# Cross-attention over 1024 context rows: the values' projection applied after the probabilities instead of before

## The chip, the cores and the metric

The kernel runs on one core of a Trainium2 chip. The time is device microseconds of one execution. Before the change the median of three runs is 3087.88 us (3087.36 to 3091.29). A core has five engines with instruction queues of their own: PE (matrix products; its loads of stationary operands are listed as PEld), DVE (vector), ACT (scalar functions), POOL (general) and SP (here it issues transfers). Work from one engine to another is ordered by semaphores. PE writes into PSUM (eight banks of 128 partitions by 512 float32 numbers); DVE and ACT take the results out.

## The reference, cut to what matters

A network of twelve blocks on x (16 batches of 64 tokens by 256). The tenth, the one changed, lets the 64 latents of a batch attend to 1024 context rows of 192 numbers and to the 64 latents themselves, in 4 heads of 64:

```python
def _L3_xattn_ref(x, latents, mask, ln_x_g, ln_x_b, ln_l_g, ln_l_b, qn_g, kn_g, Wq, Wkv, Wlkv, Wo, bo):
    ...
    xn = layernorm(x, ln_x_g, ln_x_b)          # x: the context, 16 x 1024 x 192
    ln = layernorm(latents, ln_l_g, ln_l_b)    # 16 x 64 x 256
    q = ln @ Wq.T
    kv = jnp.concatenate([xn @ Wkv.T, ln @ Wlkv.T], axis=1)
    k, v = (kv[..., :INNER], kv[..., INNER:])  # INNER = 256
    q, k, v = (split_heads(q), split_heads(k), split_heads(v))
    qn = rmsnorm(q, qn_g) * SCALE
    kn = rmsnorm(k, kn_g)
    attn = jnp.einsum('bhid,bhjd->bhij', qn, kn)
    ...                                        # masked context keys are left out
    attn = jax.nn.softmax(attn, axis=-1)
    out = jnp.einsum('bhij,bhjd->bhid', attn, v)
    out = out.transpose(0, 2, 1, 3).reshape(b, m, INNER)
    ...                                        # times Wo, plus bo; added to the stream
```

## The kernel before, in words

All numbers are float32. Blocks follow one another; `ffn2` (from line 2711) stands ahead of the changed block `xattn3` (from line 1689), `attn3` behind it. `context_weights` (line 1659) is called at the start of `ffn2`: it fetches the 192 x 512 weight wx of keys and values, forms bx (the layernorm's shift times the weight, one row repeated on all partitions), scales the weight by the layernorm's gain and takes its mean over rows away, so that a context row times wx, times the row's inverse deviation, plus bx is the projection of the normalised row. The inverse deviations of all context rows, `rctx`, were left by an earlier block.

`xattn3` loops over the 16 batches. One pass handles the softmax and values of batch b and prepares the keys and values of batch b+1:
- `scores` multiplies the 64 queries of each head with transposed keys `kT`, in three pieces (512 keys, then the 128 latents' places, then the other 512). `least` (DVE) adds the mask and finds the minimum; ACT takes the exponential with its sum and then multiplies by the reciprocal sum (`pr`, 128 x 1152 for each of two pairs of heads c).
- `project(b, j)`, four groups j a batch, makes keys and values of 2 x 128 context rows: two products with 128 stationary rows and two with 64 (the other context columns; the two halves of the array side by side), each 512 wide: 256 for keys, 256 for values. DVE (scalar_tensor_tensor) takes each half out into `kk` and `vv`, times rctx plus bx.
- `square` (ACT), `roots` (a sum on DVE, then two instructions on POOL, lines 1761 and 1762) and `scale` (DVE) normalise each group of keys; p0, p1, p2 and late are the states of groups 0 to 3.
- `keys_T` transposes a group on PE (tile `ptk`) and ACT copies it to kT; group 3 of batch b+1 is transposed only after the first scores of the next pass. `latents` (product `pkl` once per two batches, copies on POOL, line 1787) and `latents_T` do the same for the latents' own keys and values.
- `probs_T` transposes the probabilities on PE (`ptp`, two banks for each c) and ACT copies them to `pT`; `last_T` (`pto`) does so for the latents' places. `values` multiplies `vv` with `pT`: 9 key tiles x 4 heads, products 64 wide. ACT copies the result `po` to `oT`, and `output` multiplies with Wo for two batches at once, in passes of even b from 2 on, and after the loop.

The order of work on PE, DVE and ACT is the program's own: instructions recorded through `self.mm`, `self.tr`, `dve` and `act` carry an order dependency on the one before them on that engine (`in_order`, line 189). POOL's and SP's orders, and DVE instructions of the next block, are placed by the scheduler of the framework. Helpers record all of them, so the profile shows line 205 for products, 208 for transposes and 72 for DVE and ACT. Passes 1 to 3 also make the queries of later batches. `mid` holds 7 PSUM banks in rotation, `ps_o` one.

## Time and profile before

| | |
|---|---|
| median of the runs | 3087.88 us |
| profiled execution | 3099.52 us, span 3097.5 us, mean clock of PE 0.963 |
| PE, DVE, ACT, POOL busy, share of the span | 94%, 63%, 43%, 24% |
| changed block | from 2433.3 us (first pkv) to 2825.0 us (last sum into X) |
| its passes, from first scores to first scores | 29.5 us for b = 0; 24.1 to 24.7 for b = 1 to 3; 21.7 to 22.8 after |
| last pass, from first scores | 18.7 us |

A row of the order of time or of the chain of waits gives start, length, engine, line, operation, output <- inputs, partitions x elements and how many instructions are merged. Idle time before an instruction and what ended it stand in brackets. In a row of groups the last columns are total busy time, mean duration in ns, and idle time before with its releaser. In a row of windows come the length, then for PE, PEld, DVE, ACT and POOL the busy time with the number of instructions, then PE's granted clock, the share of the transfer engines and GB/s. Instructions of DVE and ACT overlap a little: one of 0.68 us lets the next start after some 0.6.

### The profile page before, as it was taken

The numbers are of one execution on the slowest core, as the hardware profiler recorded it, in microseconds if no ns is written. First come the engines' busy times: TensorE is split into PE (matmuls) and PEld (weight loads), VectorE is DVE, ScalarE is ACT, GpSimd is POOL, SyncE is SP. The second block draws the span as 40 slices with busy tenths as digits, with TensorE's granted clock in tenths as the row PEclk, the third lists the DMA queues.
The fourth block names the chain that finished last, engine by engine and source line by source line (L and its number), as shares of the span: only waits on it lengthen the run. The fifth ranks groups of instructions, "written<-read, shape, count | busy, mean of one in ns | idle before, by whom it ended". The sixth has DMA issues, their size and how long they took to land.

```text
span 3097.5 us, 66367 instructions
## 1 busy us (share of the span) xinstructions
PE 2901.7 (94%) x27980; PEld 1819.7 (59%) x27980; DVE 1952.1 (63%) x4054; ACT 1329.3 (43%) x3041; POOL 731.1 (24%) x817
## 2 busy tenths in 40 slices
PE   8999999899999999977988999998989899998888
PEld 4666666666455554456874555546976455455677
DVE  6888886523766664972127877767884677775521
ACT  3555554511554451002324444438851255554322
POOL 1000002400110001014430100024871355552132
PEclk9999999999999999988999999998998999999889
DMA  2100000013223323026762222101111111110143
GB/s 77 32 32 31 24 22 19 17 32 101 64 73 101 99 60 83 1 69 242 295 235 69 73 71 76 60 22 40 49 58 31 64 58 65 62 55 15 61 145 125
DMA packets 75824, 225.28 MB, mean 73 GB/s; under 512 B 17415, under 2 KB 30586, under 8 KB 68616
## 3 DMA queue, kind: packets, MB, share of 16 engines
q1 hardware_dynamic: 47536, 115.57, 12.0%
q0 software_dynamic: 21744, 99.34, 9.4%
q10 hardware_dynamic: 6248, 6.14, 0.7%
q8 instruction: 221, 3.62, 0.5%
q14 instruction: 75, 0.61, 0.1%
HBM read 210.09 MB, written 14.49 MB: 73 GB/s over the span
## 4 chain that ended last, share of the span: by engine, by line
PE 80%; DVE 10%; ACT 4%; DMA 2%; issue 2%; POOL 2%; SPq 0%; DVEq 0%; POOLq 0%; ACTq 0%
PE pss L205 15%; PE o L205 13%; PE pu L205 8%; PE pd L205 7%; PE psp L205 6%; PE pkv L205 5%; PE pst L208 4%; PE psc L205 3%; PE po L205 2%; DVE h L72 2%; PE psq L205 2%; PE psy L205 1%; PE pg L205 1%; PE ptp L208 1%; DVE nm L72 1%
## 5 line engine op out<-in xcount | busy, mean ns | idle before, releaser
L205 PE MATMUL pss<-cT,qw 128*32 128x256 f32 x8192 | 367.7, 385 | 18.7 <-ACT pr L72 18.6
L72 DVE TENSOR_REDUCE nm<-pss 128x2 f32<-128x512 f32 (+1 forms) x384 | 309.3, 861 | 82.7 <-PE pss L205 82.7
L205 PE MATMUL o<-pT,cx 128*64 128x512 f32 (+3 forms) x1088 | 351.7, 576 | 0.0
L72 ACT ACTIVATE pr<-pss,nmm 128x256 f32<-128x256 f32 x512 | 234.8, 485 | 161.5 <-DVE nmm L72 161.5
L205 PEld LDWEIGHTS pss<-cT,qw 128*32 128x32 f32 x8192 | 203.5, 109 | 148.4 <-ACT pr L72 26.1
L205 PEld LDWEIGHTS o<-pT,cx 128*64 128x64 f32 (+1 forms) x1088 | 134.3, 163 | 188.4 <-issue 161.8
L222 POOL TENSOR_SCALAR rs<-mv 128x8 f32<-128x8 f32 (+3 forms) x50 | 9.7, 194 | 974.7 <-DVE mv L238 511.7
L72 ACT ACTIVATE pr<-pr,sm 128x256 f32<-128x256 f32 x256 | 109.1, 497 | 203.9 <-DVE sm L72 203.9
L205 PE MATMUL pkv<-wx,cT 128*128 128x512 f32 (+1 forms) x512 | 193.1, 630 | 0.6 <-issue 0.6
L72 DVE TENSOR_SCALAR pr<-pr,sm 128x256 f32<-128x256 f32 (+1 forms) x384 | 170.1, 485 | 6.6
L1555 POOL TENSOR_TENSOR h<-h,cb 128x1024 f32<-128x1024 f32 x64 | 149.5, 2376 | 38.2 <-DVE h L72 37.2
L205 PE MATMUL pd<-wd,hT 128*128 128x256 f32 x656 | 151.5, 382 | 2.6 <-DVE hT L2754 1.4
L72 DVE TENSOR_TENSOR_SCAN h<-dA,pb 128x512 f32<-128x512 f32 x128 | 146.5, 1202 | 10.8 <-PE pb L205 7.4
L72 DVE STREAM_TRANSPOSE pT<-pr 128x1024 f32<-128x1024 f32 x128 | 151.8, 1224 | 2.2
L2531 DVE TENSOR_SCALAR y<-pd,row 128x256 f32<-128x256 f32 x39 | 18.8, 483 | 207.5 <-PE pd L205 161.8
L72 ACT ACTIVATE pr<-pss,nm 128x1024 f32<-128x1024 f32 x128 | 142.7, 1115 | 11.4 <-DVE nm L72 8.7
L208 PE MATMUL pst<-ident,pr 128*128 128x128 f32 x1024 | 140.6, 280 | 5.8 <-DVE sm L72 1.9
L208 PEld LDWEIGHTS pst<-ident,pr 128*128 128x128 f32 x1024 | 109.8, 141 | 61.5 <-ACT pT L72 26.5
L72 ACT COPY pT<-pst 128x512 f32<-128x512 f32 x128 | 75.0, 586 | 163.2 <-PE pst L208 163.2
L205 PEld LDWEIGHTS pd<-wd,hT 128*128 128x128 f32 x656 | 122.0, 190 | 30.3 <-DVE hT L2754 6.2
L205 PEld LDWEIGHTS pkv<-wx,cT 128*128 128x128 f32 (+1 forms) x512 | 64.4, 188 | 118.5 <-issue 92.6
L1762 POOL TENSOR_TENSOR rnk<-rnk,mhalf 128x8 f32<-128x8 f32 (+1 forms) x84 | 130.0, 1548 | 7.0
(570 smaller groups left out, 5803.3 us busy)
## 6 DMA issues: line engine op xcount, KB each, us to landing
cT<-in_ctxT SPq DMA_DIRECT2D x32, 768.0 KB, 4.9
cx<-in_ctxP SPq DMA_DIRECT2D x32, 768.0 KB, 4.4
cT<-in_ctxT SPq DMA_DIRECT2D x32, 512.0 KB, 4.1
cT<-in_ctxT SPq DMA_DIRECT2D x64, 256.0 KB, 5.1
offb<-d_off SPq DMA_DIRECT2D x16, 576.0 KB, 3.7
cb<-d_C SPq DMA_DIRECT2D x16, 512.0 KB, 3.9
wu<-in_L_ffn_w POOLq DMA_DIRECT2D x8, 1024.0 KB
wd<-in_L_ffn_w POOLq DMA_DIRECT2D x8, 1024.0 KB
```

The source lines that it names most:

```text
L72: ins = getattr(self.engine, op)(*args, **kwargs)
L205: self.in_order(self.nc.tensor.matmul(out, lhsT=lhsT, rhs=rhs, start=start, stop=stop))
L208: self.in_order(self.nc.tensor.transpose(out, in_, self.ident))
L222: nc.gpsimd.tensor_scalar(t[:p, :n], in_, scale, eps, ALU.mult, ALU.add)
L1555: nc.gpsimd.tensor_tensor(hs[i], hs[i], cbs[hf, g], ALU.mult)
L1762: nc.gpsimd.tensor_tensor(r, r, self.mhalf[:, : n * H], ALU.pow)
L2531: nc.vector.tensor_scalar(y[:, i, :], po[:, i * D : (i + 1) * D], weight[:, g + i : g + i + 1], None, ALU.mult)
```

## The change

Keys are projected as before, 256 wide. Values of the context are not projected. Since the softmax sum of (rctx times row times weight plus shift) is (sum of probability times rctx times row) times weight plus shift, the transposed probabilities are multiplied by rctx when they are taken out of PSUM (`probs_T`, now on DVE), and multiply the raw context rows, loaded once more in row order (`cx`, `load_cx`), in `values` (128 of the 192 columns) and `others` (64 columns, the key tiles alternating between two halves of the array). This happens one pass later, for batch b-1: `values` ahead of the second projection group, `others` after the last one. ACT copies the result of all heads to `oc`, and `heads` applies each head's 192 x 64 weights for two batches at once, adds the latents' own values (whose shift was taken away in `latents`, a subtraction on POOL) times their probabilities (`pls`), and ACT adds the shift `vb` while copying to `oT`. `vb` is made in `context_weights` by four products one column wide.

```diff
         bx = own.tile([P, 512], F32, name="bx")
-        self.wx, self.bx = wx, bx
+        vb = own.tile([P, 2], F32, name="vb")
+        self.wx, self.bx, self.vb = wx, bx, vb
         mean = own.tile([P, P], F32, name="mean")
...
             nc.scalar.copy(bx, pb)
+            pv = pool.tile([P, 512], F32, tag="m", name="pvb")
+            for c in range(2):
+                for k, n in enumerate((P, C1)):
+                    ch = slice(D + c * P, D + (c + 1) * P)
+                    self.mm(pv[:, c : c + 1], wx[:n, k, ch], self.col(f"{L}_ln_x_b", k, p=n), k == 0, k == 1)
+            nc.scalar.copy(vb, pv[:, :2])
             for k in range(2):
...
             ps_o = es.enter_context(tc.tile_pool(name=f"{L}ps_o", bufs=1, space=PSUM))
-            wx, bx = self.wx, self.bx
+            wx, bx, vb = self.wx, self.bx, self.vb
...
             qb = one.tile([P, 2, B, TQ], F32, name="qb")
-            oT = one.tile([P, 2, N], F32, name="oT")
-            kks, vvs = [], []
+            kks = []
             for i in range(2):
-                for lst, nm in ((kks, "kk"), (vvs, "vv")):
-                    x = one.tile([P, KT, H, 64], F32, name=f"{nm}{i}")
-                    nc.gpsimd.memset(x[64 - 64 * i : 128 - 64 * i, NKC], 0.0)
-                    lst.append(x)
-            ctxs, offs, kvl, st = {}, {}, {}, {}
+                x = one.tile([P, KT, H, 64], F32, name=f"kk{i}")
+                nc.gpsimd.memset(x[64 - 64 * i : 128 - 64 * i, NKC], 0.0)
+                kks.append(x)
+            ctxs, cxs, offs, kvl, vls, pTs, pls, ocs, oTs, st = ({} for _ in range(10))
...
             def square(x, n):
...
             def load(b):
...
                     ctxs[b] = self.load_ctxT(two, b)
+            def load_cx(b):
+                cxs[b] = two.tile([P, NKC, C], F32, tag="cx", name="cx")
+                nc.sync.dma_start(out=cxs[b], in_=a["ctxP"][b])
...
             def load_off(b):
...
                     act.copy(kvl[0], pl)
-                for i, dst in enumerate((kks[b % 2], vvs[b % 2])):
-                    nc.gpsimd.tensor_copy(
-                        dst[own, NKC].rearrange("p h d -> p (h d)"), kvl[0][own, i * D : (i + 1) * D]
-                    )
+                    vl = vls[b // 2] = two.tile([P, H, 64], F32, tag="vl", name="vl")
+                    nc.gpsimd.tensor_tensor(vl.rearrange("p h d -> p (h d)"), kvl[0][:, D:], bx[:, D:], ALU.subtract)
+                nc.gpsimd.tensor_copy(kks[b % 2][own, NKC].rearrange("p h d -> p (h d)"), kvl[0][own, :D])
                 return kks[b % 2][:, NKC : NKC + 1], 1
...
             def project(b, j):
...
                 c0, c1 = ctxs[b]
-                kk, vv = kks[b % 2], vvs[b % 2]
-                pp = [mid.tile([P, 512], F32, tag="m", name="pkv") for _ in range(2)]
+                kk = kks[b % 2]
+                pp = [mid.tile([P, 512], F32, tag="m", name="pk") for _ in range(2)]
                 for n in range(2):
                     jj = 4 * n + j
-                    self.mm(pp[n], c0[:, jj * P : (jj + 1) * P], wx[:, 0, :], True, False)
+                    self.mm(pp[n][:, :D], c0[:, jj * P : (jj + 1) * P], wx[:, 0, :D], True, False)
                 for n in range(2):
                     r = slice(n * 64, (n + 1) * 64)
-                    self.mm(pp[n], c1[r, j * P : (j + 1) * P], wx[r, 1, :], False, True)
+                    self.mm(pp[n][:, :D], c1[r, j * P : (j + 1) * P], wx[r, 1, :D], False, True)
                 for n in range(2):
-                    for i, dst in enumerate((kk, vv)):
-                        jj = 4 * n + j
-                        dve.scalar_tensor_tensor(
-                            dst[:, 2 * j + n].rearrange("p h d -> p (h d)"),
-                            pp[n][:, i * D : (i + 1) * D],
-                            self.rctx[:, b, jj : jj + 1],
-                            bx[:, i * D : (i + 1) * D],
-                            ALU.mult,
-                            ALU.add,
-                        )
+                    jj = 4 * n + j
+                    dve.scalar_tensor_tensor(
+                        kk[:, 2 * j + n].rearrange("p h d -> p (h d)"),
+                        pp[n][:, :D],
+                        self.rctx[:, b, jj : jj + 1],
+                        bx[:, :D],
+                        ALU.mult,
+                        ALU.add,
+                    )
                 return kk[:, 2 * j : 2 * j + 2], 2
...
             def turn(pt, at, x):
...
-            def last_T(prs):
+            def last_T(b, prs):
+                pls[b] = two.tile([P, 2, P], F32, tag="pl", name="pl", bufs=3)
                 pt = mid.tile([P, 512], F32, tag="m", name="pto")
...
                     turn(pt, c, prs[c][:, S:])
-                act.copy(st["pT"][:, :, NKC, :], pt[:, : 2 * P].rearrange("p (c q) -> p c q", c=2))
+                act.copy(pls[b], pt[:, : 2 * P].rearrange("p (c q) -> p c q", c=2))
...
             def scores(b, lo, hi):
...
-            def probs_T(c, pr):
+            def probs_T(b, c, pr):
+                if c == 0:
+                    pTs[b] = two.tile([P, NKC, 2, P], F32, tag="pT", name="pT")
+                r = self.rctx[:, b, :].rearrange("p (n j) -> p j n", n=2)
                 for jh in range(2):
...
                         turn(pt, j, pr[:, (4 * jh + j) * P : (4 * jh + j + 1) * P])
-                    act.copy(st["pT"][:, c, 4 * jh : 4 * jh + 4, :], pt.rearrange("p (j q) -> p j q", q=P))
-            def values(b, c):
-                for j in range(KT):
-                    for h in range(2):
-                        u = (h ^ c) * TQ
-                        self.mm(
-                            st["po"][h * 64 : (h + 1) * 64, c * TQ : (c + 1) * TQ],
-                            vvs[b % 2][:, j, 2 * c + h, :],
-                            st["pT"][:, c, j, u : u + TQ],
-                            j == 0,
-                            j == KT - 1,
-                        )
+                    dve.tensor_tensor(
+                        pTs[b][:, 4 * jh : 4 * jh + 4, c, :].rearrange("p (j n) q -> p j n q", n=2),
+                        pt.rearrange("p (j n q) -> p j n q", j=2, n=2),
+                        bc(r[:, 2 * jh : 2 * jh + 2], 3, P),
+                        ALU.mult,
+                    )
+            def tile_of(b, k):
+                return cxs[b][:, 4 * (k % 2) + k // 2], pTs[b][:, k].rearrange("p c q -> p (c q)")
+            def values(b):
+                st["o"] = ps_o.tile([P, 2, 2 * P], F32, tag="o", name="o")
+                for k in range(NKC):
+                    cx, pT = tile_of(b, k)
+                    self.mm(st["o"][:, 0, :], cx[:, :P], pT, k == 0, False)
+            def others(b):
+                for k in range(NKC):
+                    cx, pT = tile_of(b, k)
+                    self.mm(st["o"][k % 2 * 64 : k % 2 * 64 + 64, 1, :], cx[:, P:], pT, False, k >= NKC - 2)
+                if b % 2 == 0:
+                    ocs[0] = one.tile([P, 2, 2 * H // 2, 2, TQ], F32, tag="oc", name="oc")
+                act.copy(ocs[0][:, :, :, b % 2, :], st["o"].rearrange("p i (h q) -> p i h q", q=TQ))
+            def heads(m):
+                po = mid.tile([P, 512], F32, tag="m", name="poh")
+                po = po[:, : 2 * P].rearrange("p (c q) -> p c q", c=2)
+                for c in range(2):
+                    for i in range(2):
+                        for hh in range(2):
+                            h = 2 * c + hh
+                            self.mm(
+                                po[hh * 64 : hh * 64 + 64, c, :],
+                                wx[:, i, D + h * 64 : D + (h + 1) * 64],
+                                ocs[0][:, i, 2 * c + (hh ^ c)].rearrange("p b q -> p (b q)"),
+                                c == 0 and i == 0,
+                                False,
+                            )
+                for c in range(2):
+                    for bb in range(2):
+                        for hh in range(2):
+                            u = (hh ^ c) * TQ
+                            self.mm(
+                                po[hh * 64 : hh * 64 + 64, c, bb * TQ : (bb + 1) * TQ],
+                                vls[m][:, 2 * c + hh, :],
+                                pls[2 * m + bb][:, c, u : u + TQ],
+                                False,
+                                c == 1 and bb == 1,
+                            )
+                oT = oTs[m] = two.tile([P, 2, P], F32, tag="oT", name="oT")
+                for c in range(2):
+                    act.activation(oT[:, c], po[:, c], AF.Identity, bias=vb[:, c : c + 1])
...
             def output(t):
...
                 for c in range(2):
-                    self.mm(ps[:, :D], oT[:, c, t * P : (t + 1) * P], wo[:, c, :], c == 0, c == 1)
+                    self.mm(ps[:, :D], oTs[t][:, c, :], wo[:, c, :], c == 0, c == 1)
                 dve.tensor_tensor(self.X[:, t, :], self.X[:, t, :], ps[:, :D], ALU.add)
...
             for b in range(B):
...
                 load(b + 2)
+                load_cx(b)
                 load_off(b + 1)
...
                 sums = self.small.tile([P, 2], F32, tag="sums", name="sums")
-                st["po"] = ps_o.tile([P, 2 * TQ], F32, tag="o", name="po")
                 pss = scores(b, 0, 512)
...
                     p0, lat = roots(*p0), roots(*lat)
+                if b > 0:
+                    values(b - 1)
                 dve.reciprocal(sums[:, 0:1], sums[:, 0:1])
...
                     late = project(b + 1, 3)
-                st["pT"] = one.tile([P, 2, KT, P], F32, tag="pT", name="pT")
-                probs_T(0, prs[0])
+                if b > 0:
+                    others(b - 1)
+                probs_T(b, 0, prs[0])
                 if more:
                     keys_T(b + 1, 0, act.copy)
-                last_T(prs)
+                last_T(b, prs)
                 if more:
                     late = square(*late)
-                probs_T(1, prs[1])
+                probs_T(b, 1, prs[1])
                 if more:
...
                     keys_T(b + 1, 1, act.copy)
+                if b % 2 == 0 and b > 0:
+                    heads(b // 2 - 1)
                 if 1 <= b <= 3:
                     scale(*q)
-                values(b, 0)
-                values(b, 1)
                 if more:
...
                     scale(*late)
-                act.copy(oT[:, :, b * TQ : (b + 1) * TQ], st["po"].rearrange("p (c q) -> p c q", c=2))
                 if 1 <= b <= NT:
                     nc.gpsimd.tensor_tensor(self.X[:, b - 1, :], self.X[:, b - 1, :], row, ALU.add)
+            values(B - 1)
+            others(B - 1)
+            heads(NT - 1)
             output(NT - 1)
```

## The prediction

> **What bounds the kernel now.** I read the page first (PE busy 94%), then the busy time by windows over the changed block (2433 to 2825 us), then its chain of waits, then the order of time inside one batch. Two neighbouring batches by windows (length; then busy PE, PEld, DVE, ACT, POOL; clock), with batch 0:
>
> ```profile
> 2458.90:2488.40 29.50, 25.36 (x174) 12.93 (x173) 21.12 (x55) 13.71 (x24) 15.73 (x18) 0.87 0.14 48
> ...
> 2628.40:2651.20 22.80, 22.55 (x173) 11.34 (x172) 16.45 (x44) 12.24 (x21) 10.95 (x14) 1.00 0.18 61
> 2651.20:2672.90 21.70, 21.64 (x173) 11.21 (x172) 15.56 (x40) 13.16 (x24) 10.66 (x11) 1.00 0.18 66
> ```
>
> PE is full at full clock; the pair takes 44.5 us. The chain of waits from batch 4 on is nearly all PE:
>
> ```profile
> 2652.83 2.78 PE pkv L205 x8
> 2655.61 1.24 PE pss L205 x16
> 2656.85 8.92 PE pkv L205 x24
> 2665.77 1.02 PE ptp L208 x8
> ```
>
> So a projection group is 2.78 or 2.97 us of path. But behind the last of them PE meets DVE and POOL just in time (order of time; brackets are idle time and its releaser):
>
> ```profile
> 2646.94 0.68 DVE L72 TENSOR_TENSOR kk<-kk,rnk 128x512 f32<-128x512 f32 x1
> ...
> 2647.76 0.63 PE L208 MATMUL ptk<-ident,kk 128*128 128x128 f32 x4
> ...
> 2647.96 0.69 DVE L72 TENSOR_REDUCE rnk<-sq 128x8 f32<-128x512 f32 x1 [0.34 <-ACT sq L72]
> ...
> 2649.43 1.66 POOL L1762 TENSOR_TENSOR rnk<-rnk,mhalf 128x8 f32<-128x8 f32 x1
> ...
> 2651.13 0.69 DVE L72 TENSOR_TENSOR kk<-kk,rnk 128x512 f32<-128x512 f32 x1 [1.89 <-POOL rnk L1762]
> ...
> 2652.18 0.66 PE L208 MATMUL ptk<-ident,kk 128*128 128x128 f32 x4
> ```
>
> Key group 1 is transposed 0.14 us after its scaling ended, group 3 about 0.4 us after: no slack stands between DVE's chain and PE.
>
> **PE, part by part.** A call is two records (256 pkv calls, 512 records). Half-width projections have a twin in the first block, 16 records of width 256 (full rows, then paired half rows) in 2.89 us, to the next start:
>
> ```profile
> 303.59 2.96 PE L205 MATMUL psp<-wv,cT 128*128 128x256 f32 x16
> 306.48 1.10 PE L205 MATMUL o<-pT,v 128*32 128x64 f32 x64
> ```
>
> That is 12 passes of 0.2145 and 0.32 of changes; ours has 6 passes, 1.29. The group of 2.97 holds 6 passes of 0.429 and 0.40 of changes, so ours is 1.69 (1.62 for group 0, 1.5 for group 1, which will follow a full-row group). Four groups fall from 2.87 + 8.92 = 11.79 (starts to starts) to 6.50: -5.29 per batch.
>
> The new values and others have a twin in the folded blocks, 24 records of width 512 in 7.22 us: 8 full ones 3.63, 16 paired ones 3.59.
>
> ```profile
> 811.60 7.29 PE L205 MATMUL o<-pT,cx 128*128 128x512 f32 x24
> 818.82 1.09 PE L208 MATMUL psT<-ident,xn 128*128 128x128 f32 x8
> ```
>
> At width 256: values, 16 passes of 0.2145 + 0.2 = 3.63; others, 8 pair passes + 0.18 = 1.90. They replace 72 narrow records, 2.25. heads: 16 paired records by the folded blocks' head product (32 records in 1.8) 0.9, 16 narrow ones at 2.25/72 each 0.5, a change 0.1: 1.5 per two batches. PE alone gains 5.29 + 2.25 - 3.63 - 1.90 - 0.75 = 1.26 us per batch.
>
> **DVE.** Eight vv instructions go (0.39 from start to start, 3.1 us); four evacuations of 128x512 from PSUM, moved from ACT, come. Nearest row, a product read from PSUM:
>
> ```profile
> L72 DVE TENSOR_TENSOR zs<-py,zs 128x512 f32<-128x512 f32 x8 | 5.4, 675 | 3.7 <-PE py L1577 3.7
> L72 DVE TENSOR_TENSOR y<-y,zs 128x512 f32<-128x512 f32 x8 | 7.0, 869 | 0.3
> ```
>
> I take 0.675, 0.61 start to start as for the kk product; ends 0.67 and 0.87. Busy time falls 0.7 us; what matters is the place. The evacuations wait for ptp, and queued behind them on DVE are scale(p1), the sum of late, scale(p2) and scale(late), for which PE's ptk 1, 2 and 3 and POOL's roots wait. Laid out from T, the end of the last projection (0.2 us from PE to DVE):
> - others end T+1.90. The first ptp is readable at 2.55; two evacuations to 3.77. PE does ptp, ptk 0 (0.43), pto (0.22) and the third ptp; readable at 4.13; two evacuations to 5.35; scale(p1) to 5.96; ptk 1 starts 6.10. PE was free at 4.57: wait 1.5.
> - The sum of late ends 6.56, scale(p2) 7.17, ptk 2 starts 7.30: wait 0.75 in odd batches, covered in even ones by heads (6.56 to 8.06).
> - POOL (0.34 + 1.7) delivers late at 8.8; scale(late) to 9.44; ptk 3 ends 10.0 in odd batches. Even: ACT copies the head sums by 8.83 (two of 0.27), output to 9.71, its DVE sum (0.34) at 9.93, scale(late) to 10.88, ptk 3 ends 11.5.
>
> Before, this stretch takes 7.80 (2644.87 to 2652.67) and 8.89 (2665.70 to 2674.59): +2.2 odd, +2.6 even. The stretch from ptk 3 to T changes by 3.63 - 5.29 = -1.66; softmax there has ready time to spare (its last product ends 2643.1, ptp starts 2644.87, and pto now comes later after T).
> Sum for batches 4 to 14: 6 x 0.94 + 5 x 0.54 = +8.3.
>
> **Edges.** Batches 1 to 3 (queries; stretch 8.5 to 9.2 before, set by POOL): +1.5, +2.3, +1.5 less 3 x 1.66: +0.3. Batch 0: its group 0 ran 4.56 at a low clock (2463.07 to 2467.63), half as long -2.0; two vv instructions fewer ahead of the minima -0.8; its last group 3.58, shorter by 1.3; then a stretch of 8.15 by the same layout without others, against 7.56 (2482.36 to 2489.92), +0.6: -3.5. Prologue: eight vv instructions fewer, less a POOL subtraction (128x256 row 0.74) ahead of the kk latent copy: -1. End: now 2.95 (po) and 1.15 (output) after the transposes; then 3.63 + 1.90 + copy 0.8 + heads 1.5 + copies 0.8 + output 1.2, starting 1.5 earlier because values(14) and others(14) fill PE's 6.02 us of idleness and keep it warm: +3.9. The bias product in the block before: eight records at the half clock there (the gate's 16 take 3.21), 1.6, and a scaling of 0.49 it no longer hides: +2.2.
>
> **At no cost.** values(b-1) stands ahead of groups 1 to 3 on PE; the -1.66 counts that, and DVE, which takes their results, idles for them before too. The one bank for o is emptied by ACT 20 us before its next use. ACT loses four 0.53 copies and gains one. SP issues 16 more loads (0.33 each; 12.6 MB, the folded blocks' twin lands in 4.4 us): load_cx(b) waits for others(b-2), load_off(b+1) may queue behind it, but both are used about 20 us later; without that cover, 4.4 us a batch. The POOL subtraction in odd batches delays the latents' square by 0.74, ahead of exp on ACT; exp's input comes 1.5 us later still. Dropped POOL copies and memsets were off the path.
>
> **Sum.** 8.3 + 0.3 - 3.5 - 1 + 3.9 + 2.2 = +10 us, against the profiled execution's 3099.52 (span 3097.5, 2.0 around it): 3109.7. That execution lies 11.6 above the median 3087.88, so the median goes to 3098.
>
> **Clock.** Batch 0, with PE idle for 2.25 us at one ptk after longer idling, has 0.87; batches with waits under 0.5 us have 1.00. My waits of 1.5 and 0.75 lie between; I take 1.00, being nearer the latter by share of a batch. At 0.87 the worst end is 13% of some 20 us: 2.6 us a batch.
> The Trainium skill's "TensorE: Matmul & The Clock Gate", section "A second HAM failure mode: psum-queue depth-cycling", speaks against this change: frequent small idling between groups lets the clock oscillate to half. By its window of 3.4 us, once in each of 14 batches, an estimate from that page is 24 us more; its table of rules allows gaps below about 3 us, by which nothing is added.
>
> **Rivals.** (1) Faster: the DVE waits vanish because scale(p1) is not held up, so PE alone counts. Odd batches -2.0, even -0.5; batches 1 to 14 -18, edges +1.6: 3072. For it: PE is 99% busy now. Against: the queue order is fixed, and scale(p1) already ends 0.14 us before its reader. It decides once ptk 1 starts more than 0.7 us sooner than T+6.10. (2) About nothing: half of those waits covered: 3087. (3) Slower still: evacuations at the 0.87 row push ptk 1 by 0.5, +7 over 14 batches; with the clock lowered in a third of the batches, another +10: 3115. (4) PE groups gain less, since weights (0.19 a load) hardly fit under 0.2145 passes: 0.1 on each of eight groups a pair, +5; within my range.
>
> **How the numbers follow.** Forecast 0.5 (3090 to 3106), rival 1 0.2, rival 2 0.12, rival 3 0.18. Measurement tells about 0.2%, 6.2 us. Faster: rival 1, 0.18 and a little of 2: 0.2. Same: the rest of 2 and the low end of the forecast: 0.22. Slower: 0.58. The range reaches to both outer cases, 3074 to 3115.
>
> **What would show it.** Right: pkv half as wide at 0.21 per pass; PE idle before ptk 1 and 3 released by DVE kk; DVE pT rows near 0.68; steady pair about 46 us. Wrong: no idle there and a pair near 42; pT rows over 0.8; clock below 0.95 in 2630 to 2670.

## The result, and the profile after

The changed kernel takes 3115.83 us (median of 5 runs, 3106.20 to 3118.26), the kernel before, run beside it, 3088.25 us (5 runs, 3087.36 to 3097.18). The ratio of the two kernels' runs is 1.0072, with a 95% interval of 1.0055 to 1.0089 (the quotient of the two medians, 1.0089, lies at its upper end): the change makes the kernel slower by some 0.7%. The prediction was 3098 us, with a range of 3074 to 3115. The median lies just above that range; the ratio, applied to the 3087.88 us that the prediction started from, gives 3110 us.

The profiled execution of the changed kernel took 3115.58 us (span 3113.9 us, mean clock of PE 0.96). PE is busy for 2894.2 us in it, 93% of the span. First the busy time by windows of the changed kernel, from first scores to first scores: batch 0, two undisturbed neighbours (the passes of batches 7 and 8, with PE's clock at 1.00), and the pass of batch 6.

```profile
2457.90:2484.95 27.05, 19.30 (x101) 11.74 (x101) 20.48 (x51) 11.86 (x20) 14.71 (x18) 0.74 0.15 52
...
2632.82:2655.46 22.64, 20.57 (x130) 13.24 (x129) 15.84 (x39) 11.10 (x18) 9.61 (x13) 1.00 0.28 96
2655.46:2679.09 23.63, 21.28 (x162) 14.58 (x161) 15.01 (x36) 12.27 (x21) 10.44 (x11) 1.00 0.27 93
2608.64:2632.82 24.18, 22.77 (x162) 15.24 (x161) 15.11 (x36) 12.27 (x21) 10.39 (x11) 0.93 0.27 90
```

Before, PE worked 22.55 of 22.80 us and 21.64 of 21.70. Now it works 20.57 of 22.64 and 21.28 of 23.63: it has 2.34 us less to do in the pair (the prediction said 2.5), and it stands idle for 4.4 us of the pair, against 0.3 before. The undisturbed pair is 46.27 us, against 44.47. The last line is a third thing: the same work as the line above it, 0.55 us longer, at a clock of 0.93.

The chain of waits of the changed kernel, behind the last projection of the pass of batch 7 ("issue" lines and short pieces are left out):

```profile
2647.64 1.88 PE o L205 x16
2649.52 1.02 PE ptp L208 x8
...
2651.67 0.47 DVE pT L72
...
2652.88 0.68 DVE kk L72
2653.56 0.61 DVE rnk L72
...
2654.24 0.63 POOL rnk L1766
...
2654.95 1.67 POOL rnk L1767
...
2656.64 0.70 DVE kk L72
...
2657.48 0.63 PE ptk L208 x4
```

Before, this chain held nothing but PE in these passes. Now it leaves PE at the transposed probabilities and goes through DVE (an evacuation, the scaling of key group 1, the sum of group 3), POOL (two instructions of the root) and DVE again (the scaling of group 3), and only then back to PE. The order of time of the same stretch shows what PE waited for.

```profile
2650.14 1.29 DVE L72 TENSOR_TENSOR pT<-ptp,rctx 128x512 f32<-128x512 f32 x2 [0.65 <-PE ptp L208]
...
2651.67 1.29 DVE L72 TENSOR_TENSOR pT<-ptp,rctx 128x512 f32<-128x512 f32 x2 [0.24 <-PE ptp L208]
...
2653.70 0.63 PE L208 MATMUL ptk<-ident,kk 128*128 128x128 f32 x4 [1.41 <-DVE kk L72]
...
2654.90 0.63 PE L208 MATMUL ptk<-ident,kk 128*128 128x128 f32 x4 [0.56 <-DVE kk L72]
...
2657.48 0.63 PE L208 MATMUL ptk<-ident,kk 128*128 128x128 f32 x4 [0.93 <-DVE kk L72]
```

These are the waits that the prediction laid out, at 1.41 us ahead of key group 1 for its 1.5, 0.56 us ahead of group 2 in odd batches for its 0.75, and 0.93 us ahead of group 3. Four evacuations in two pairs of 1.29 us stand ahead of the scaling of group 1 in DVE's queue.

### The profile page after: what moved, and what is told of

Read it like the earlier page. It is cut to its first block, busy times and chain, and to the rows that moved or that the text cites. A ratio compares the mean times of both kernels' runs of the same rounds, so it can differ in the third digit from the quotient of the medians.

```text
span 3113.9 us, 65420 instructions
## 1 busy us (share of the span) xinstructions
PE 2894.2 (93%) x27604; PEld 1869.9 (60%) x27604; DVE 1944.1 (62%) x3990; ACT 1312.5 (42%) x2994; POOL 719.2 (23%) x807
## 4 chain that ended last, share of the span: by engine, by line
PE 80%; DVE 11%; ACT 3%; POOL 2%; issue 2%; DMA 2%; DVEq 0%; SPq 0%; POOLq 0%; ACTq 0%
PE o L205 15%; PE pss L205 14%; PE pu L205 8%; PE pd L205 7%; PE psp L205 6%; PE pst L208 4%; PE psc L205 3%; PE pk L205 3%; DVE h L72 2%; PE psq L205 2%; PE psy L205 1%; PE pg L205 1%; DVE nm L72 1%; PE po L205 1%; PE pb L205 1%
## 5 line engine op out<-in xcount | busy, mean ns | idle before, releaser
L205 PE MATMUL o<-pT,cx 128*64 128x512 f32 (+3 forms) x1600 | 442.3, 515 | 0.4 <-issue 0.4
L205 PEld LDWEIGHTS o<-pT,cx 128*64 128x64 f32 (+1 forms) x1600 | 198.5, 163 | 219.2 <-issue 179.9
L208 PEld LDWEIGHTS pst<-ident,pr 128*128 128x128 f32 x1024 | 110.5, 142 | 62.2 <-ACT pT L72 25.8
L205 PEld LDWEIGHTS pu<-xT,up 128*128 128x128 f32 x736 | 111.2, 193 | 21.1 <-ACT hT L2583 14.6
L205 PE MATMUL pu<-xT,up 128*128 128x128 f32 x736 | 121.6, 291 | 0.7 <-ACT hT L2583 0.5
```

Source lines behind the costliest of these rows:

```text
L205: self.in_order(self.nc.tensor.matmul(out, lhsT=lhsT, rhs=rhs, start=start, stop=stop))
L208: self.in_order(self.nc.tensor.transpose(out, in_, self.ident))
```

## The experiments

Three theories were set against each other first. Q: the order in DVE's queue costs the time (the evacuations hold up the scalings). L: the added loads hold it up. P: the new products on PE are dearer than laid out. A fourth, C, came from the trace: short waits also lower PE's clock.

One table for all runs. "Block" is the traced time from the start of the last products of the `po` tile in the block before (2302.97 us in the kernel before, 2301.45 in the changed one) to the first transposes of the block behind (2825.01 and 2841.34); "pair" is two neighbouring passes at a clock of 1.00 (in e4, where such passes do not lie side by side, one of each kind). Each run has 4 to 10 executions, e4 only two; the kernel before beside them has 17 to 25.

| run | block, us | pair, us | ratio to before (95%) |
|---|---|---|---|
| before | 522.0 | 44.47 | 1 |
| changed | 539.9 | 46.27 | 1.0072 (1.0055 to 1.0089) |
| e1 evacuations on ACT | 518.8 | 43.8 | 0.9999 (0.9987 to 1.0011) |
| e2 keys first | 506.7 | 41.93 | 0.9971 (0.9957 to 0.9985) |
| e3 `others` late | 524.0 | 44.13 | 1.0019 (1.0006 to 1.0032) |
| e4 before, evacuations on DVE | 566.2 | 49.3 | 1.0154 (1.0116 to 1.0193) |
| e5 two loads only | 539.9 | 46.27 | 1.0076 (1.0054 to 1.0098) |
| e6 e2, bias by transposes | 501.0 | 41.92 | 0.9938 (0.9921 to 0.9954) |
| e7 scaling of group 1 first | 523.9 | 44.07 | 1.0015 (1.0002 to 1.0029) |
| e8 filled waits | 536.1 | 46.14 | 1.0053 (1.0032 to 1.0073) |
| e9 before, keys first | 520.0 | 45.01 | 0.9989 (0.9974 to 1.0003) |
| e10 changed again | 539.5 | 46.27 | 1.0065 (1.0048 to 1.0082) |
| e11 filled again | 535.8 | 46.14 | 1.0048 (1.0032 to 1.0064) |

### e1: the evacuations on ACT

```diff
-                    dve.tensor_tensor(
-                        pTs[b][:, 4 * jh : 4 * jh + 4, c, :].rearrange("p (j n) q -> p j n q", n=2),
-                        pt.rearrange("p (j n q) -> p j n q", j=2, n=2),
-                        bc(r[:, 2 * jh : 2 * jh + 2], 3, P),
-                        ALU.mult,
-                    )
+                    act.copy(pTs[b][:, 4 * jh : 4 * jh + 4, c, :], pt.rearrange("p (j q) -> p j q", q=P))
```

> The changed kernel with the probabilities taken out of PSUM by ACT again, as plain copies; the product with rctx is left out. Theory Q (queue order: on DVE the four evacuations wait for PE and hold back scale(p1), the sum of late, scale(p2) and scale(late)): PE's waits of 1.4 us before ptk 1 go, those before ptk 3 shrink; laid out with the durations of the changed kernel's profile, a steady pair goes from 46.3 to 43.4 us and the time falls by some 18 us, to the kernel before (ratio to it 0.997 to 1.003). Rival L (the 16 added loads, or their queue, cost the time) and rival P (the new products on PE are dearer than the sum has them): no change, ratio 1.007, pair 46.3.

Measured: 3091.96 us, ratio 0.9999, pair 43.8 us (43.4 expected). With the four evacuations out of DVE's queue the whole loss is gone, while the loads and the wide products are all still there. That speaks for Q and against P and L.

### e2: the keys first

Nothing is left out here; only the order on DVE, ACT and POOL behind the last projection is another.

```diff
                     late = project(b + 1, 3)
+                    scale(*p1)
+                    late = roots(*square(*late))
...
                 last_T(b, prs)
                 if more:
-                    late = square(*late)
+                    scale(*p2)
                 probs_T(b, 1, prs[1])
                 if more:
-                    scale(*p1)
-                    late = roots(*late)
-                    scale(*p2)
                     latents_T(b + 1)
```

> The changed kernel, everything computed, with another order on DVE and ACT: scale(p1), the square and the sum of late directly behind the last projection, ahead of the evacuations, and scale(p2) between the two pairs of evacuations. Theory Q: PE meets its keys ready; laid out as before, a pair takes 41.8 us instead of 46.3, 27 us less in all, so 5 to 9 us under the kernel before (ratio 0.996 to 1.000), and PE's clock stays at full speed in the steady batches. Rivals L and P: ratio stays 1.007.

Measured: 3085.10 us, ratio 0.9971, pair 41.93 us. It is faster than both kernels. Its windows, two neighbouring passes:

```profile
2618.01:2638.70 20.69, 20.34 (x129) 13.26 (x128) 15.27 (x39) 11.17 (x18) 10.37 (x13) 1.00 0.30 102
2638.70:2659.94 21.24, 21.09 (x161) 14.59 (x161) 15.42 (x37) 12.33 (x21) 8.91 (x10) 1.00 0.32 106
```

PE works 41.43 of 41.93 us: it is the bound again, with less to do. The order of time behind the last projection of the first of these passes, which ends at 2632.83:

```profile
2634.67 0.68 DVE L72 TENSOR_TENSOR kk<-kk,rnk 128x512 f32<-128x512 f32 x1
...
2636.12 1.28 DVE L72 TENSOR_TENSOR pT<-ptp,rctx 128x512 f32<-128x512 f32 x2
...
2637.32 0.68 DVE L72 TENSOR_TENSOR kk<-kk,rnk 128x512 f32<-128x512 f32 x1
2637.38 0.60 PE L208 MATMUL ptk<-ident,kk 128*128 128x128 f32 x4
...
2638.14 0.63 PE L208 MATMUL ptk<-ident,kk 128*128 128x128 f32 x4 [0.16 <-DVE kk L72]
```

The scaling of group 1 is done at 2635.35, before PE turns to that group, and group 3's sum (between it and the first evacuations) reaches POOL 3.46 us after the last projection (2636.29) instead of 6.67 (2654.24) in the changed kernel; the 0.9 us for which DVE is idle in the changed kernel's rows (0.65 ahead of the first pair of evacuations and 0.24 ahead of the second) is put to use. The waits of 1.41 and 0.56 us are down to none and 0.16.

### e3: `others` behind the transposes of the latents

```diff
-                if b > 0:
-                    others(b - 1)
                 probs_T(b, 0, prs[0])
...
                     latents_T(b + 1)
+                if b > 0:
+                    others(b - 1)
+                if more:
                     keys_T(b + 1, 1, act.copy)
```

> The changed kernel with others(b-1) moved on PE from behind the last projection to behind latents_T, into the wait before ptk 1, and its copy on ACT with it. DVE's order is as in the changed kernel. Theory Q: the wait before ptk 1 is filled and the evacuations start 1.9 us sooner; by the layout a pair takes 43.7 us and the time falls by 15 us (ratio 1.001 to 1.004). Rivals L and P: 1.007, since the same work is done on PE.

Measured: 3099.35 us, ratio 1.0019 as expected, pair 44.13 us (43.7 expected). PE's own work (1.9 us) now lies where it waited for DVE; what is left of the waits comes behind it (0.35, 0.47 and 0.99 us after an odd batch). PE's order covers about two of the four idle microseconds, DVE's order removes them.

### e4: the kernel before with its evacuations on DVE

```diff
-                    act.copy(st["pT"][:, c, 4 * jh : 4 * jh + 4, :], pt.rearrange("p (j q) -> p j q", q=P))
+                    dve.tensor_copy(st["pT"][:, c, 4 * jh : 4 * jh + 4, :], pt.rearrange("p (j q) -> p j q", q=P))
```

> The kernel before with one part of the change alone: the four evacuations of the transposed probabilities moved from ACT to DVE, as plain copies. Theory Q: the layout of the kernel before with this one move gives 48.5 us for a pair instead of 44.5, 25 to 36 us more in all (ratio 1.008 to 1.012). Rivals L and P: about nothing, since neither a load nor a product is added (DVE has 6 us of idle time per batch).

Measured: 3141.00 us (two executions), ratio 1.0154. The sign is as expected and the size is not: a pair was to take 48.5 us; an undisturbed pass of each kind make 49.3, and neighbouring passes take 50.6 us and more. Windows of this kernel, from first scores to first scores:

```profile
2567.16:2591.25 24.09, 21.64 (x169) 11.21 (x168) 17.64 (x44) 11.58 (x21) 10.43 (x11) 1.00 0.17 58
2591.25:2617.95 26.70, 24.06 (x170) 12.68 (x169) 19.38 (x48) 10.40 (x17) 11.28 (x14) 0.94 0.15 53
...
2694.14:2719.31 25.17, 22.53 (x170) 11.32 (x169) 20.91 (x52) 10.41 (x17) 12.54 (x16) 1.00 0.16 56
```

The first and third lines make the undisturbed pair. The second and third are passes of the same kind; one has PE's clock at 0.94 and is 1.5 us longer. Where the drop begins can be read in the order of time:

```profile
2663.82 0.73 PE L208 MATMUL ptk<-ident,kk 128*128 128x128 f32 x4 [2.45 <-DVE kk L72]
...
2688.55 1.08 PE L208 MATMUL ptk<-ident,kk 128*128 128x128 f32 x4 [2.45 <-DVE kk L72]
```

Behind a wait of 2.45 us four transposes take 0.73 or 1.08 us instead of 0.63. So moving the evacuations alone, with keys and values projected as before, is enough to lose the time, and theory C has to be added to Q.

### e5: two loads of the raw context only

```diff
             def load_cx(b):
-                cxs[b] = two.tile([P, NKC, C], F32, tag="cx", name="cx")
-                nc.sync.dma_start(out=cxs[b], in_=a["ctxP"][b])
+                if b < 2:
+                    cxs[b] = two.tile([P, NKC, C], F32, tag="cx", name="cx")
+                    nc.sync.dma_start(out=cxs[b], in_=a["ctxP"][b])
+                else:
+                    cxs[b] = cxs[b % 2]
```

> The changed kernel, with the raw context rows loaded for batches 0 and 1 only; later batches weight the rows of those two again, so 14 loads of 0.79 MB and their issues on SP are left out, and the values of batches 2 to 15 are those of other rows. Theory Q (order on DVE): the loads lie beside other work, nothing changes: ratio to the kernel before 1.004 to 1.008, steady pair 46.2 us, the idle time of 1.4 us ahead of key group 1's transposes stays. Theory L (the added loads hold the passes up): the ratio falls by 0.002 or more below the changed kernel's 1.0072 and the pair by 1 us or more.

Measured: 3122.33 us, ratio 1.0076; pair 46.27 us and block 539.9 us, both as in the changed kernel to 0.1 us. The 14 transfers left out cost nothing that can be measured. Theory L is out.

### e7: only the scaling of group 1 first

```diff
                     late = project(b + 1, 3)
+                    scale(*p1)
...
                 if more:
-                    scale(*p1)
                     late = roots(*late)
```

> The changed kernel with one instruction moved per batch: the scaling of key group 1 goes ahead of the four evacuations on DVE; the sum of group 3 and the scaling of group 2 stay behind them. Theory Q, laid out from durations: the wait ahead of key group 1's transposes goes, those ahead of groups 2 and 3 stay or grow by some tenths; steady pair 43.6 to 44.6 us, ratio to the kernel before 1.000 to 1.004. Theory P (the products themselves are dearer): pair 46, ratio 1.006.

Measured: 3101.99 us, ratio 1.0015, pair 44.07 us. One instruction moved per batch brings back most of the loss, and the next link shows in its place. The order of time in an odd batch:

```profile
2653.60 0.63 PE L208 MATMUL ptk<-ident,kk 128*128 128x128 f32 x4 [1.57 <-DVE kk L72]
2654.16 1.09 PE L205 MATMUL pss<-kT,qb 64*64 64x512 f32 x8
2656.18 0.63 PE L208 MATMUL ptk<-ident,kk 128*128 128x128 f32 x4 [0.93 <-DVE kk L72]
```

Group 1 is in time, group 2 is now waited for 1.57 us and group 3 0.93 us as before. Q holds link by link; theory P (46 us) falls.

### e8, e10, e11: the waits filled, beside the changed kernel

Transposes without use keep PE working while it waits; DVE's order, and so the moment at which the scaled keys are there, stays.

```diff
-            def keys_T(b, j, copy):
+            def keys_T(b, j, copy, fill=0):
...
                 pt = mid.tile([P, 512], F32, tag="m", name="ptk")
+                for _ in range(fill):
+                    turn(pt, 0, pair(b, 0, 0))
...
-                keys_T(b, 3, act.copy)
+                keys_T(b, 3, act.copy, 5 if b % 2 == 0 and b > 0 else 0)
...
-                    keys_T(b + 1, 1, act.copy)
+                    keys_T(b + 1, 1, act.copy, 8 if b > 0 else 0)
...
-                    keys_T(b + 1, 2, act.copy)
+                    keys_T(b + 1, 2, act.copy, 3 * (b % 2))
```

> The changed kernel with transposes of no use (of key group 0, into the place that the real ones then overwrite) where PE would stand idle: 8 ahead of key group 1's own, 3 ahead of group 2's after odd batches, 5 ahead of group 3's in even passes from 2 on; at 0.137 us each 1.1, 0.4 and 0.7 us, less than the waits of 1.4, 0.56 and 0.93. DVE's order is that of the changed kernel. If the short waits are what lowers the clock in batches 1 to 14: no stretch at half clock between 2485 and 2840 us of the span, passes 1, 2, 3, 6 and 12 as long as the others of their kind (22.6 and 23.6, 1 to 3 with the queries 24.5 to 25), ratio 1.003 to 1.006. If the lowered clock has another cause: the same half-clock stretches, ratio 1.007 or more.

> The changed kernel as it is, beside the filled one on the same chip, to set their times against each other. If the half-clock stretches cost what the traces show (3.9 us in batches 1 to 14), this one is 0.0010 to 0.0020 of the time longer than the filled one: ratio to the kernel before 1.006 to 1.008.

> The filled waits once more, beside the changed kernel on the same chip: ratio to the kernel before 1.0045 to 1.006, and 3 to 6 us under the changed kernel's median; no stretch at half clock in batches 1 to 14. If the two differ by less than 1 us, the lowered clock costs nothing that a time shows.

Measured: e8 3113.62 us, ratio 1.0053; on one chip side by side e10 3115.70 us (1.0065) and e11 3108.15 us (1.0048). The ratios are as expected; the medians differ by 7.6 us, more than the 3 to 6 expected, but the intervals of the two ratios overlap, so the times alone don't settle the size; the traces do. Windows of e10, the passes of batches 2, 4, 6 and 8:

```profile
2509.96:2535.31 25.35, 23.93 (x174) 16.61 (x173) 16.30 (x38) 14.05 (x24) 11.55 (x13) 0.97 0.26 87
2561.05:2584.43 23.38, 21.96 (x161) 14.67 (x160) 15.11 (x36) 12.36 (x21) 9.38 (x11) 0.97 0.27 93
2607.15:2631.31 24.16, 22.74 (x161) 15.24 (x160) 15.10 (x36) 12.26 (x21) 10.35 (x11) 0.93 0.26 91
2653.95:2677.58 23.63, 21.29 (x162) 14.58 (x161) 15.01 (x36) 12.27 (x21) 10.43 (x11) 1.00 0.28 93
```

and of e11, the same passes:

```profile
2508.10:2533.29 25.19, 24.74 (x187) 17.91 (x186) 16.20 (x38) 14.09 (x25) 12.29 (x13) 1.00 0.26 87
2558.32:2581.49 23.17, 22.72 (x174) 15.98 (x173) 15.01 (x36) 12.40 (x22) 10.11 (x11) 1.00 0.30 94
2604.07:2627.64 23.57, 22.91 (x175) 15.98 (x174) 15.01 (x36) 12.27 (x21) 10.51 (x11) 1.00 0.29 94
2650.22:2673.78 23.56, 22.90 (x174) 15.97 (x173) 15.01 (x36) 12.27 (x21) 10.50 (x11) 1.00 0.27 92
```

With PE kept working the clock is 1.00 throughout, and the pass of batch 6 is as long as that of batch 8. (The passes of batches 1 and 2 stay a little longer than expected, 25.8 and 25.2 us in e8.) The block is 3.7 us shorter in e11 than in e10, and 3.8 us shorter in e8 than in the changed kernel. Not all of it is the clock's: the undisturbed pair, too, is 0.13 us shorter with the filling (46.27 to 46.14), which makes 0.9 us in 14 batches. C's share is some 3 us; the rest of the 17.9 us is not the clock's.

### e9: the kernel before with the keys first

The edit is that of e2, made in the kernel before.

> The kernel before with the order of the keys-first run: scaling of key group 1 and the sum of group 3 right behind the last projection, scaling of group 2 between the two pairs of evacuations (which stay on ACT here). If PE alone bounds batches 4 to 14 of the kernel before, the order has nothing to give: steady pair 44.2 to 44.6 us, batches 1 to 3 shorter by at most 0.5 us each (PE waits 0.48 us for POOL's roots there), ratio 0.998 to 1.001; then what the keys-first run gains is the change's. If the kernel before loses time to the same order, its pair falls towards 43 and the ratio to 0.994.

Measured: 3092.25 us, ratio 0.9989 with an interval that includes 1; the pair is 45.0 us, 0.5 longer than before rather than the same (why stays open). In the kernel before the order has nothing to give, so what e2 gains over it is the change's own saving on PE, once DVE's order lets it through.

### e6: the bias column by transposes

On top of e2, the four one-column products in `context_weights` (eight records) are replaced:

```diff
-            pv = pool.tile([P, 512], F32, tag="m", name="pvb")
-            for c in range(2):
-                for k, n in enumerate((P, C1)):
-                    ch = slice(D + c * P, D + (c + 1) * P)
-                    self.mm(pv[:, c : c + 1], wx[:n, k, ch], self.col(f"{L}_ln_x_b", k, p=n), k == 0, k == 1)
-            nc.scalar.copy(vb, pv[:, :2])
...
             late = square(*late)
+            pv = mid.tile([P, 512], F32, tag="m", name="pvb")
+            for c in range(2):
+                turn(pv, c, bx[:, D + c * P : D + (c + 1) * P])
+            for c in range(2):
+                act.copy(vb[:, c : c + 1], pv[:, c * P : c * P + 1])
             scale(*lat)
```

> The order of the keys-first run, and the bias column vb taken from the row bx by two transposes in the prologue of the changed block, where PE stands idle, instead of by eight one-column products in the block before. If those products cost what the traces show (2.3 us between the two bias products and the mean), the block before returns to its old length and the time lies about 2 us below the keys-first run: ratio 0.9955 to 0.9975, span of the block before shorter by 2 to 3 us, steady pair 41.9 us. If the wait for the weight's transfer swallows them, nothing is gained: 0.997 to 0.998.

Measured: 3077.71 us, ratio 0.9938 (0.9921 to 0.9954), the fastest of all. It gains more than the 2 us expected. In the changed kernel the order of time in `context_weights` is

```profile
2316.69 4.05 PE L205 MATMUL pbx<-wx,bk 128*128 128x512 f32 x4 [8.17 <-DMA wx<-in_L_xattn_WkvT]
2320.67 2.12 PE L205 MATMUL pvb<-pcol,wx 128*128 128x1 f32 x8
2322.95 4.05 PE L205 MATMUL pmx<-wx,mean 128*128 128x512 f32 x4 [0.16 <-DVE wx L1687]
```

so the products and the scaling behind them put 2.28 us between the two neighbours. From `po` to the first projection of the changed block e2 takes 133.5 us and e6 129.0, 4.5 us less; 2.3 of these stand in the rows above. Another 2.1 lie in the gate products and the first products behind them, which are the same in both kernels. Windows from the first gate product to the first `pu`, of e2 and of e6:

```profile
2330.72:2343.30 12.58, 12.58 (x42) 9.23 (x41) 3.49 (x13) 3.41 (x4) 1.50 (x2) 0.54 0.07 21
2329.20:2339.64 10.44, 10.44 (x42) 6.90 (x41) 4.47 (x14) 3.41 (x4) 1.51 (x2) 0.67 0.09 25
```

PE is full in both, at a clock of 0.54 and 0.67: in e2 it stays at half clock for 30.7 us in the block before, in e6 for 23.9. The changed block gains too. Its batch 0 is 1.8 us shorter in e6 (window of its pass):

```profile
2454.64:2478.73 24.09, 16.71 (x102) 10.61 (x101) 19.54 (x51) 11.71 (x19) 15.75 (x18) 0.91 0.17 58
```

The clock is 0.91 there, instead of 0.73 in e2; this run does not tell whether the two transposes in PE's idle time of the prologue did that. From `po` on, the traces of e2 and e6 differ by 5.6 us; the ratios differ by 0.0033, some 10 us, and the rest is not found in them.

## Where the prediction was right, and where it was off

The forecast was +10 us in the trace, put on a median of 3087.88. The median came out 17.8 us above 3098. Of these, 11.6 are the reference point: the profiled execution of before, 3099.52 us, was held to lie 11.6 us above its kernel's median, and this was taken off; the changed kernel's profiled execution (3115.58) lies at its median. The medians of the kernel before beside the experiments were 3092.56, 3095.80 and 3091.76 us (17 to 25 runs each, 3084.88 to 3104.54), 4 to 8 us above the three runs that the prediction had; those were three chips, so how much of this is the chip's and how much chance is not shown. The profiled execution was a long one of its kernel: the block before ran 27.3 us at half clock in it, and 23.9 in e4 and e9, where that block is the same. The other 6 us are in the sum: the profiled times differ by 16.1 us instead of 10.2.

Term by term, from the two traces (the stretches add up to the 17.9 us of the table; the work ahead of them was 1.5 us shorter in the profiled execution after):

| term | predicted | measured | read from (before to after) |
|---|---|---|---|
| block before | +2.2 | +3.3 | 130.32 to 133.58, `po` to first projection |
| prologue | -1 | -2.7 | 25.61 to 22.87, to first scores |
| batch 0 | -3.5 | -1.5 | 31.02 to 29.54, to the end of key group 3's transposes |
| batches 1 to 3 | +0.3 | +3.5 | 73.81 to 77.35 |
| batches 4 to 14 | +8.3 | +11.5 | 244.38 to 255.85 |
| end | +3.9 | +3.8 | 16.90 to 20.70 |

**Right: the mechanism.** Ptk 1 starts at T+6.13 (predicted 6.10), with a wait of 1.41 (1.5); ptk 2 waits 0.56 in odd batches and not in even ones (0.75 and none). The even stretch is 11.45 (11.5), the undisturbed pair 46.27 (about 46). The stretch from ptk 3 to T is 13.08 after 14.75 in odd batches, -1.67 (-1.66). One evacuation takes 0.682 us:

```profile
L72 DVE TENSOR_TENSOR pT<-ptp,rctx x64: 678/682/693, 2479.8 to 2831.0; 128x512 f32<-128x512 f32 x64
```

The first projection group takes 1.59 from start to start (1.62), values 3.56 (3.63), others 1.88 (1.90), heads 1.49 (1.5). The end came out to 0.1 us, with some luck: the terms named for it add up to +4.2, not +3.9. Loads at no cost: e5 confirms it. One reading was off without harm: the bank of `o` is emptied some 10 us before its next use (2650.2 to 2660.8), not 20.

**Failed: "I take 1.00" for the clock.** The waits of 1.5 and 0.75 were put with the batches of waits under 0.5. In the changed kernel PE runs at half clock for about 3.4 us at a time behind four of the odd batches (1, 3, 5 and 11), and in e10 behind the same four. With the waits filled this is gone, and some 3 us with it. It explains about half of the miss in batches 1 to 3 (their stretches are 11.40, 11.81 and 11.45 us at the granted clock, and 10.58, 11.75 and 10.58 in e8: 1.75 us, of which the filling itself makes 0.2) and half of that in batches 4 to 14 (11.47 less 11 undisturbed batches of +0.90: 1.6).

**Failed by size: the odd stretch.** 10.0 was laid out, 10.38 came: POOL's first instruction of the root took 0.62 us there rather than the 0.34 that was entered, so group 3's scaling started at T+9.07 and not at 8.8. (In the trace of before that instruction takes 0.62 us at the same place, 2648.73, behind 1.07 us of POOL's idleness, and 0.25 where POOL is not idle; the 0.34 stands for neither.) That is 0.38 in each of five batches, 1.9 us in 4 to 14. **Batches 1 to 3** were entered at +1.5, +2.3 and +1.5 a stretch; at full clock (e8) they are +2.07, +2.67 and +2.07, 1.5 us more in all, and the clock's 1.75 comes on top.

**Failed by size: batch 0.** Group 0 fell from 4.56 to 2.85 (-1.7, entered as -2.0), the last group from 3.58 to 2.87 (-0.7, entered as -1.3, because PE was at low clock behind 4.07 us of idleness), the stretch behind it rose from 7.56 to 8.50 (+0.9, entered as +0.6). The -0.8 entered ahead of the minima did not come: up to group 0 batch 0 became 0.4 us longer, from there to the last group 0.4 us shorter. The prologue gave more than its -1.

**Failed by size: the bias products.** 2.28 us stand between the neighbours (2.2 was entered), but the way to the changed block is 133.4 to 133.7 us in every run with these products and 128.9 to 129.0 without them in e4, e6 and e9: some 4.5 us, of which about 2 are the lowered clock behind them. The +3.3 of the table is less only because the profiled execution of before was a long one there (130.3).

**The rivals.** Rival 1 (PE alone counts) was to decide from a start of ptk 1 more than 0.7 us ahead of T+6.10, and ptk 1 started at T+6.13. Its arithmetic was right all the same: -2.0 and -0.5 make -2.5 a pair, and e2, where the scaling of group 1 is not held up, has a pair 2.54 us shorter. Rival 2 (half covered) is what e3 and e7 look like: 0.15 to 0.2% slower. Rival 3 named the measured 3115 us, but half for a cause that is not there: evacuations at 0.87 us (they take 0.682). Its other half, a clock lowered in a third of the batches, is there in four of fourteen, at some 3 us instead of 10. Rival 4 (weight loads under short passes) is not there: three groups take 4.88 us, which is 1.5 and twice 1.69.

The prediction weighed two places of the Trainium skill's "TensorE: Matmul & The Clock Gate" against each other. What its section "A second HAM failure mode: psum-queue depth-cycling" says, that frequent small idling lets the clock oscillate, is borne out in part: four windows in fourteen batches, some 3 us instead of the 24 of the prediction's estimate from that page. The table in "Why this matters for your kernels" warns of gaps above about 3 us only, and that is too weak for this case: no wait ahead of the keys' transposes in these batches is longer than 1.42 us.

## What to carry to other kernels

Moving an evacuation to another engine moves it into that engine's queue: lay out what stands behind it and who waits for that, since a saving on the bounding engine (here 2.5 us a pair) arrives only if the next engine's order lets it. Here the same work in another order on DVE turned 0.7% slower into 0.3% faster, and a column taken by two transposes from a row that was there anyway into 0.6% (of this last step the traces show 5.6 us, 0.2%). And take the reference point from more than three runs where less than a per cent matters.

## What the runs showed of the hardware

Waits much shorter than the stretch that they slow can lower PE's clock. The order of time of the changed kernel behind batch 1:

```profile
2508.38 0.63 PE L208 MATMUL ptk<-ident,kk 128*128 128x128 f32 x4 [1.42 <-DVE kk L72]
2509.57 1.09 PE L208 MATMUL ptk<-ident,kk 128*128 128x128 f32 x4 [0.57 <-DVE kk L72]
2510.45 1.06 PE L208 MATMUL ptq<-ident,q 128*128 128x128 f32 x4
2511.44 1.77 PE L205 MATMUL pss<-kT,qb 64*64 64x512 f32 x8
```

After 1.42 and 0.57 us of idleness with 0.6 us of work between them, four transposes take 1.09 instead of 0.63 us, and the first scores 1.77 instead of 1.09. The same two waits behind batch 7 (1.41 and 0.56) change nothing.

What picks the batches can be read from the granted clock. All half-clock stretches of the changed kernel in and around the block last 3.41 us or a multiple of it, and they start on one grid with that step: behind batches 1, 3, 5 and 11 at 2509.47, 2560.67, 2608.45 and 2748.40, which are 15, 14 and 41 steps apart. Windows of one step each, with the waits behind batch 1 and the step that follows them, and the two steps over which the waits behind batch 7 are spread:

```profile
2506.06:2509.47 3.41, 1.53 (x13) 1.08 (x11) 3.17 (x7) 1.74 (x5) 1.11 (x2) 1.00 0.54 204
2509.47:2512.88 3.41, 3.31 (x16) 1.88 (x16) 1.25 (x2) 1.43 (x3) 2.00 (x2) 0.50 0.00 2
...
2649.41:2652.82 3.41, 2.88 (x26) 2.60 (x24) 2.52 (x5) 2.27 (x5) 1.39 (x1) 1.00 0.98 355
2652.82:2656.24 3.42, 1.97 (x16) 1.05 (x16) 1.93 (x4) 1.17 (x2) 1.91 (x2) 1.00 0.15 61
```

Behind batch 1 nearly all of the idleness falls into one step, 1.88 of 3.41 us, and the next step runs at half clock. Behind batch 7 a step ends within the first wait, which leaves 0.53 us in one step and 1.45 in the other, and the clock stays. It is so in all three traces with these waits (changed, e5, e10): each of the twelve half-clock stretches in batches 1 to 14 follows a step in which PE was idle for 1.82 to 1.99 us, and no other step there has more than 1.64. With the waits filled (e8, e11) no step from the middle of batch 1 on has more than 0.70, and none is slowed. In e1 (at most 1.77) and e3 (1.58) the clock is 1.00 in these batches; in e7 one step of 2.03 us, as batch 1 begins, is followed by half clock, and those behind it, of at most 1.77, are not; in e4 eight steps of 2.00 to 2.46 us are each followed by half clock, and one of 1.95 is not. So in these runs the limit lies between some 1.8 and 2 us of idleness within one step, and the length of a single wait does not decide. The batches hit are the same in the three traces because the grid lies at the same place relative to the block, to 0.4 us, though the block began 1.4 us sooner in the span of e10 and 8.3 us later in that of e5; why it does so is not shown.
